# A macaron stack of four mixtures and attentions on one core: the first mixture's choices written in program order on every compute engine, and the bias table's row and pieces moved

## The chip, the cores and the metric

The kernel runs on one core of a Trainium2 chip. The metric is the device time of one execution in microseconds (us), the median of several runs; smaller is better. A core has five engines that run side by side and meet at semaphores: TensorE (PE in the profile; its weight loads are PEld), VectorE (DVE), ScalarE (ACT), GpSimd (POOL) and SyncE (SP), which issues most transfers. ScalarE and GpSimd can issue transfers too; all transfers are carried by the same 16 DMA engines.

## What is computed

The reference is a stack of four layers, each with a half-weighted feed-forward part, an attention part and a second half-weighted feed-forward part, on x of shape 4 x 512 x 128. The change touches the first feed-forward part and the preparation of the attention that follows it. Cut to these:

```python
def _L0_ffn_ref(inputs, gate_w, w1, b1, w2, b2):
    tokens = inputs.reshape(-1, d_model)
    capacity = int(np.ceil(CAP_FACTOR * T / num_experts))
    logits = jnp.einsum('td,ed->te', tokens, gate_w)
    probs = jax.nn.softmax(logits, axis=-1)
    expert_idx = jnp.argmax(probs, axis=-1)
    mask = jax.nn.one_hot(expert_idx, num_experts)
    ranks = jnp.cumsum(mask, axis=0) - 1.0
    keep = (ranks < capacity) * mask
    sec_mask = jax.nn.one_hot(ranks.astype(int), capacity) * keep[:, :, None]
    combine_weights = probs[:, :, None] * sec_mask
    dispatch = jnp.einsum('tec,td->ecd', sec_mask, tokens)
    h = jax.nn.relu(jnp.einsum('ecd,edh->ech', dispatch, w1) + b1[:, None, :])
    expert_out = jnp.einsum('ech,ehd->ecd', h, w2) + b2[:, None, :]
    return jnp.einsum('tec,ecd->td', combine_weights, expert_out)

# attention of layer 0: a bias table by distance, 16 heads
table = rel_pos_emb.reshape(2 * MAX_LEN - 1, H, D).sum(axis=-1)
bias = transpose(table[rel_idx]); att = q k / sqrt(D) + bias; causal softmax; att v

x = x + 0.5 * _L0_ffn_ref(_layernorm(x), ...)
x = x + _L0_attn_ref(_layernorm(x), ...)
x = x + 0.5 * _L0_ffn_ref(_layernorm(x), ...)
# layers 1 to 3 follow
```

So each token is normalised, chooses one of 8 experts, and gets the next free row of that expert, up to a capacity of 320.

## The kernel before

The kernel is written in a tile language: the author writes instructions on engines, and a scheduler puts the instructions of each engine into one fixed order and adds the waits. Within a `manual_schedule` block the engines named there keep the order of the program text. After the build each engine works through its own list in order, so an instruction that waits holds everything behind it on that engine. Transfers that SP issues go into one queue, and likewise those of ScalarE.

Four batches of 512 tokens (`NB`, `S`) lie in fast memory as four tiles of 128 tokens each (`NT`). The first mixture, `f00`, is an object of class `Mixture`:

- `empty` (L288) fills the rows of the dispatch buffer `disp_f` in device memory with zeros, `clear` (L293) the result rows `res_f`; both are transfers of SP (`spread_zeros`, L284).
- `tokens` (from L296) is a generator for one batch: statistics on VectorE (`norms`, L168 and L169), reciprocal root on GpSimd (L172, L173, and L176, L177 for the offset when ScalarE or GpSimd scales), the scaled rows (L182 on ScalarE, L186 on VectorE), a turn on TensorE (L195) with its copy (L321 or L134), the logits (L330), then the choice: maximum (L344), exponentials (L348), mask (L228 to L234), running count (L362), ranks on TensorE (L373, L375, L379), gate factor (L385 to L389), and the row number `to` (L400 to L409). Last, GpSimd copies the factor into the row (L413) and scatters the rows of four tiles to `disp_f`, one indirect transfer for each tile (L416). L307 writes the tokens' own numbers into a column of each row. It is used by every mixture of the kernel, in later stages too.
- `experts` (from L426) fetches an expert's rows (`fetch`, L447), turns them (L466) with a copy on ScalarE (L468), makes the list of places to send results to (L472, L475 on VectorE), multiplies by `w1` (L490), adds the bias and clips on ScalarE (L494) and VectorE (L495), multiplies by `w2` (L526), adds `b2` (L506), weights the rows (L511) and scatters them (L512). Expert e + 2 is fetched and e + 1 prepared while e is computed; an optional `beside` is called once for each expert.

`prep_table` (from L1012) makes the bias table of attention 0, again as a generator with three stops: it loads `rel` (L1016); sums it, turns it on TensorE (L1024), writes a row `tab_row` and stores it in device memory as `tab_rows` (L1032); then, for eight pairs of heads, loads a shifted piece `rev` (L1038, buffers shared under the name "raw", five of them), turns it with TensorE (L1043) and copies it into `table`. `copy` (L131) alternates between VectorE (L134) and ScalarE (L136). The left part of `table` is filled with zeros (L1020). `prep_l0_attn` loads and turns the attention's weights (L144 to L147, L976 to L988), and `padded_values` fills two value buffers `vpad` on GpSimd (L585, L586). `first_weights` loads the experts' weights in eight transfers (L563, L564) and turns the bias `b1` (L570, copied at L571 into `b1T`).

At the top of the program these are called in this order: the table's first stop, the fill of `disp_f`, four steps of batch 0's choice, the table's second stop, all weights, the fill of `res_f`, the rest of the choices with a lag of two steps between batches, the table's pieces, the attention weights, the value buffers, the experts. Batches 0 and 2 are scaled by ScalarE, 1 and 3 by VectorE. No block gives an order there; the scheduler does. Attention 0 (`l0_attn`) follows the experts and has its order written out.

Of the kernel before, what the change touches and what calls it, by code (L numbers as in the profile page):

```python
# [17 lines left out]
P = 128  # L18
D = 128
NB, S = 4, 512  # L20
# [3 lines left out]
E = 8  # L24
# [17 lines left out]
def kernel(ctx: ExitStack, tc: tile.TileContext, a: dict, out: bass.AP):  # L42
    nc = tc.nc
# [9 lines left out]
    def const(shape, name, dtype=FP):  # L53
        return cpool.tile(shape, dtype, name=name, tag=name)

    def bank(name):
        return psum.tile([P, 512], FP, name=name, tag="bank", bufs=8)
# [7 lines left out]
    xs = [const([P, NT, D], f"x{b}") for b in range(NB)]  # L65
# [58 lines left out]
    def load_row(ap, name, tag=None):  # L124
        t = pools["w"].tile([P, D], FP, name=name, tag=tag or name)
        nc.sync.dma_start(t, ap.partition_broadcast(P))
        return t
# [3 lines left out]
    def copy(dst, src):  # L131
        n_copies[0] += 1
        if n_copies[0] % 2:
            nc.vector.tensor_copy(dst, src)  # L134
        else:
            nc.scalar.copy(dst, src)  # L136
# [23 lines left out]
    def norms(srcs, dsts, tag, on="vector", fine=False):  # L160

        g = len(srcs) * NT
        st = small.tile([P, g, 6], FP, name=f"st_{tag}", tag=f"bn_st{g}")
        mv = small.tile([P, g, 2], FP, name=f"mv_{tag}", tag=f"bn_mv{g}")
        rs = small.tile([P, g], FP, name=f"rs_{tag}", tag=f"bn_rs{g}")
        rstd = small.tile([P, g], FP, name=f"rstd_{tag}", tag=f"bn_rstd{g}")
        for t in range(g):
            nc.vector.bn_stats(st[:, t, :], srcs[t // NT][:, t % NT, :])  # L168
            nc.vector.bn_aggr(mv[:, t, :], st[:, t, :])  # L169
            if fine and t % 2 and t < g - 1:  # L170
                yield
        nc.gpsimd.tensor_scalar(rs, mv[:, :, 1], EPS, None, ALU.add)  # L172
        nc.gpsimd.tensor_tensor(rstd, rs, mhalf[:, :g], ALU.pow)  # L173
        if on != "vector":
            off = small.tile([P, g], FP, name=f"off_{tag}", tag=f"bn_off{g}")
            nc.gpsimd.tensor_scalar(off, mv[:, :, 0], -1.0, None, ALU.mult)  # L176
            nc.gpsimd.tensor_tensor(off, off, rstd, ALU.mult)  # L177
        yield
        for t in range(g):
            src, dst = srcs[t // NT][:, t % NT, :], dsts[t // NT][:, t % NT, :]  # L180
            if on == "scalar" or (on == "both" and t % 2):
                nc.scalar.activation(dst, src, AF.Identity, bias=off[:, t : t + 1], scale=rstd[:, t : t + 1])  # L182
            elif on == "gpsimd":
                nc.gpsimd.tensor_scalar(dst, src, rstd[:, t : t + 1], off[:, t : t + 1], ALU.mult, ALU.add)
            else:
                nc.vector.tensor_scalar(dst, src, mv[:, t, 0:1], rstd[:, t : t + 1], ALU.subtract, ALU.mult)  # L186
            if fine and t % 2 and t < g - 1:
                yield
        yield
# [55 lines left out]
    class Mixture:  # L245
# [50 lines left out]
        def tokens(self, bs, wT, on="vector", pool=None, fine=False, apart=False):  # L296

            pool = pool or routing
            k, G = self.k, len(bs) * NT
            i0 = bs[0] * NT  # L300
            tag = f"{self.tag}_{bs[0]}"

            ns = [work.tile([P, NT, W + 2], FP, name=f"n_{self.tag}_{b}", tag="nm", bufs=4) for b in bs]
            rows = [n[:, :, 2 : 2 + D] for n in ns]
            for n, b in zip(ns, bs):
                for c in range(k):
                    nc.gpsimd.tensor_scalar(  # L307
                        n[:, :, 0 if c else D + 2],
                        tok_id[:, c * TILES + b * NT : c * TILES + (b + 1) * NT],
                        1.0,  # L310
                        None,
                        ALU.add,
                    )
            yield from norms([xs[b] for b in bs], rows, tag, on, fine)
            if fine:
                yield
            nTs = []
# [37 lines left out]
            if k == 2:  # L355
                rest = without(pool, pr, by_tile[0], G, -4.0, f"r{G}")
                _, second = route(pool, rest, G, f"r1{G}", by_tile[1])
# [14 lines left out]
            ps = bank(f"rank_{tag}")[:, : k * E * G]  # L372
# [7 lines left out]
            ps = ps.rearrange("p (k e g) -> p k e g", k=k, e=E)  # L380
# [202 lines left out]
    def padded(pool, i):  # L583
        v = pool.tile([P, NT, NH, SLOT], FP, name=f"vpad{i}", tag=f"vpad{i}", bufs=1)
        nc.gpsimd.memset(v, 0.0)  # L585
        nc.gpsimd.memset(v[:, :, :, HD : HD + 1].rearrange("p t h o -> p (t h o)"), 1.0)  # L586
        return v

    def padded_values(pool):
        vpads[:] = [padded(pool, i) for i in range(2)]  # L590
# [419 lines left out]
    l0 = {}  # L1010

    def prep_table(pool):  # L1012


        rel = stage.tile([P, D], FP, name="rel", tag="rel", bufs=1)
        nc.sync.dma_start(rel, a["L0_attn_rel_pos_emb"][P - 1 : 2 * P - 1, :])  # L1016
        yield

        table = pool.tile([P, NH, S], FP, name="table", tag="table", bufs=1)
        nc.vector.memset(table[:, :, : S - 2 * P], 0.0)  # L1020
        tab = stage.tile([P, NH], FP, name="tab", tag="tab", bufs=1)
        nc.vector.tensor_reduce(tab, rel.rearrange("p (h d) -> p h d", d=HD), AX.X, ALU.add)
        ps = bank("tabT")
        nc.tensor.matmul(ps[:NH, :P], tab, flip, start=True, stop=True)  # L1024
        last = stage.tile([NH, 1], FP, name="tab_last", tag="tab_last", bufs=1)
        nc.vector.tensor_copy(last, ps[:NH, 0:1])
        row = stage.tile([NH, 3 * P], FP, name="tab_row", tag="tab_row", bufs=1)
        nc.vector.memset(row[:, :P], 0.0)
        nc.vector.tensor_scalar(row[:, P : 2 * P], ps[:NH, :P], last, None, ALU.subtract)
        nc.vector.memset(row[:, 2 * P :], NEG)  # L1030
        rows = dram.tile([NH, 3 * P], FP, name="tab_rows", tag="tab_rows")
        nc.sync.dma_start(rows, row)  # L1032
        yield

        for h in range(0, NH, 2):

            rev = stage.tile([P, 2, 2 * P], FP, name=f"rev{h}", tag="raw")
            nc.sync.dma_start(  # L1038
                rev,
                bass.AP(tensor=rows.tensor, offset=rows.offset + h * 3 * P, ap=[[1, P], [3 * P, 2], [1, 2 * P]]),  # L1040
            )
            ps = bank(f"turned{h}")
            nc.tensor.matmul(ps, flip, rev.rearrange("p h s -> p (h s)"), start=True, stop=True)  # L1043
            copy(table[:, h : h + 2, S - 2 * P :], ps.rearrange("p (h s) -> p h s", h=2))
        l0["table"] = table
        yield

    def prep_l0_attn():
        qkv = head_weights(a["L0_attn_qkv_w"], a["L0_attn_qkv_b"], "l0")
        owT = load_T(a["L0_attn_proj_w"], D, D, "ow0T", "owT")  # L1050
        ob = load_row(a["L0_attn_proj_b"], "ob0", "ob")
        l0["attn"] = qkv, owT, ob
# [533 lines left out]
    def whole(parts):  # L1586
        for _ in parts:
            pass

    def skewed(gens, lag):  # L1590

        live = {i: g for i, g in enumerate(gens)}
        r = 0
        while live:
            for i in list(live):
                if r >= i * lag and next(live[i], "end") == "end":
                    del live[i]
            r += 1
            yield
# [16 lines left out]
    def first_weights():  # L1616
        l0["w"] = yield from moe_weights("L0_ffn", "l0")

    pairs = [[b, b + 1] for b in range(0, NB, 2)]
    gate0T = wpool.tile([D, E], FP, name="gate0T", tag="gate0T")  # L1620
    ps = bank("gate0T")
    nc.tensor.transpose(ps[:, :E], gate0, ident[:E, :E])
    nc.vector.tensor_copy(gate0T, ps[:, :E])
    with tc.tile_pool(name="tables", bufs=1) as tables:
        f00 = Mixture("f00", CAP0, 1)
        f00.zeroed(stage, "raw", 5)
        made = prep_table(tables)
        next(made)
        whole(f00.empty())
        with tc.tile_pool(name="routing00", bufs=2) as pool:  # L1630
            choices = [f00.tokens([b], gate0T, "vector" if b % 2 else "scalar", pool) for b in range(NB)]
            for part in choices[:1] * 4:
                next(part)
            next(made)
            whole(first_weights())
            f00.clear()
            whole(skewed(choices, 2))
        whole(made)
        prep_l0_attn()
        padded_values(tables)  # L1640
        f00.experts(l0["w"])
        f01 = Mixture("f01", CAP0, 1)

        f30 = Mixture("f30", CAP3, 2)
        l0_attn(f00.combine, emptied(f01, f30), lambda b: f01.tokens([b], gate0T, fine=True))
    with tc.tile_pool(name="weights12", bufs=1) as mid:
        pools["w"] = mid
        prep_l1()
        with tc.tile_pool(name="raw2", bufs=1) as pool:
            made = prep_l2(pool)  # L1650
# [119 lines left out]
```

## Time and profile before

| What | us |
|---|---|
| Median of 3 runs (1506.3 to 1509.8) | 1507.57 |
| The profiled execution | 1509.34 |
| Its span in the profile | 1507.4 |
| TensorE busy in the span | 1284.4 (85%) |
| VectorE busy | 873.8 (58%) |
| ScalarE busy | 686.4 (46%) |
| GpSimd busy | 691.8 (46%) |
| Mean granted TensorE clock, of 1 | 0.911 |

The first stretches of the span, in busy microseconds of each engine:

| Stretch, us | TensorE | VectorE | ScalarE | GpSimd | granted clock | DMA, GB/s |
|---|---|---|---|---|---|---|
| 0 to 20 | 1.87 | 14.03 | 4.20 | 12.63 | 1.00 | 242 |
| 20 to 40 | 15.14 | 8.69 | 2.84 | 8.25 | 1.00 | 268 |
| 40 to 60 | 11.06 | 4.23 | 1.76 | 8.09 | 0.78 | 125 |
| 60 to 80 | 19.36 | 6.78 | 7.73 | 6.19 | 0.96 | 70 |
| 80 to 100 | 20.00 | 7.01 | 9.26 | 10.21 | 1.00 | 60 |
| 100 to 120 | 8.68 | 5.98 | 3.87 | 7.96 | 0.82 | 48 |

The choices of the first mixture lie in 4 to 51 us, its experts in 62 to 112, and attention 0 begins behind them. A group of the page is named by line, engine, operation and tile; a line of the chain gives start, length and the piece of work; a line of the timeline gives start, length, engine, line, operation, tiles, and in brackets the idle time of the engine just before it and what ended that. Busy time is an average over stages: which engine sets the pace is read from the waits of a stage, not from these columns.

### The profile page before, as it was taken

The numbers are of one execution on the slowest core, as the hardware profiler recorded it, in microseconds if no ns is written. First come the engines' busy times: TensorE is split into PE (matmuls) and PEld (weight loads), VectorE is DVE, ScalarE is ACT, GpSimd is POOL, SyncE is SP. The second block draws the span as 40 slices with busy tenths as digits, with TensorE's granted clock in tenths as the row PEclk, the third lists the DMA queues.
The fourth block names the chain that finished last, engine by engine and source line by source line (L and its number), as shares of the span: only waits on it lengthen the run. The fifth ranks groups of instructions, "written<-read, shape, count | busy, mean of one in ns | idle before, by whom it ended". The sixth has DMA issues, their size and how long they took to land.

```text
span 1507.4 us, 28892 instructions
## 1 busy us (share of the span) xinstructions
PE 1284.4 (85%) x10677; PEld 828.3 (55%) x10677; DVE 873.8 (58%) x2934; ACT 686.4 (46%) x1439; POOL 691.8 (46%) x808
## 2 busy tenths in 40 slices
PE   4787999995979989998999878749599999998394
PEld 3464666674766666676656656627343434333273
DVE  5336777663345657777566655434287787772243
ACT  1235877871433367776622222104245555553041
POOL 5355767871433577876442112555502323202243
PEclk9898999996979999999999877859799999997597
DMA  8410240002412884241130000032105000000223
GB/s 259 106 53 22 80 170 13 9 5 75 146 42 58 231 257 137 93 141 31 38 76 1 1 0 3 29 91 85 49 8 184 8 12 4 16 1 15 78 82 108
DMA packets 100660, 106.21 MB, mean 70 GB/s; under 512 B 9084, under 2 KB 73832, under 8 KB 100520
## 3 DMA queue, kind: packets, MB, share of 16 engines
q1 hardware_dynamic: 91752, 90.11, 20.7%
q0 software_dynamic: 6656, 13.22, 2.5%
q8 instruction: 84, 1.38, 0.4%
q10 hardware_dynamic: 2112, 1.05, 0.3%
q14 instruction: 56, 0.46, 0.1%
HBM read 62.49 MB, written 41.85 MB: 69 GB/s over the span
## 4 chain that ended last, share of the span: by engine, by line
PE 67%; DVE 10%; POOL 7%; issue 6%; DMA 6%; ACT 2%; SPq 1%; POOLq 0%; DVEq 0%; ACTq 0%
PE s_a L621 13%; PE t_a L666 9%; PE h_f L490 5%; PE acc_a L688 5%; PE o_f L526 5%; PE acc_a L826 5%; PE y_f L1451 4%; PE t_a L621 3%; PE ot_a L845 2%; POOL res_f L512 2%; PE gate_f L1468 2%; DMA cb_f<-rows_f 2%; POOL disp_f L416 1%; PE lg_f L330 1%; PE T_f L195 1%
## 5 line engine op out<-in xcount | busy, mean ns | idle before, releaser
L653 POOL TENSOR_SCALAR sc_a<-sc_a,top_a 128x128 f32<-128x128 f32 (+3 forms) x256 | 275.9, 1093 | 87.1 <-DVE top_a L638 60.2
L621 PE MATMUL s_a<-k_a,q_a 32*128 32x512 f32 (+3 forms) x1536 | 264.1, 537 | 5.3 <-DVE top_a L642 4.5
L710 DVE TENSOR_REDUCE low<-s_a 128x1 f32<-128x512 f32 x256 | 163.0, 683 | 42.7 <-PE t_a L621 30.4
L730 ACT ACTIVATE w_a<-t_a 128x512 f32<-128x512 f32 x240 | 131.8, 596 | 108.1 <-PE t_a L621 68.7
L666 PE MATMUL t_a<-ident,sc_a 128*128 128x128 f32 x1280 | 171.3, 279 | 4.9 <-DVE top_a L642 4.1
L512 POOL DMA_INDIRECT res_f<-y_f,back_f x112 | 106.9, 954 | 129.1 <-ACT y_f L511 94.2
L666 PEld LDWEIGHTS t_a<-ident,sc_a 128*128 128x128 f32 x1280 | 142.4, 142 | 39.9 <-issue 16.6
L621 PE MATMUL t_a<-ql_a,k_a 32*128 32x512 f32 x480 | 158.8, 644 | 0.4 <-DVE low L710 0.3
L655 ACT ACTIVATE sc_a<-sc_a,top_a 128x128 f32<-128x128 f32 (+3 forms) x256 | 134.8, 576 | 15.3 <-DVE top_a L642 14.8
L621 PEld LDWEIGHTS s_a<-k_a,q_a 32*128 32x128 f32 x1536 | 93.8, 185 | 73.3 <-issue 38.4
L675 ACT ACTIVATE w_a<-t_a 128x256 f32<-128x256 f32 (+2 forms) x192 | 94.2, 526 | 68.9 <-PE t_a L666 68.5
L416 POOL DMA_INDIRECT disp_f<-n_f,to_f x96 | 94.8, 987 | 52.8 <-issue 36.9
L526 PE MATMUL o_f<-w_l,h_f 128*128 128x128 f32 (+1 forms) x896 | 110.4, 278 | 1.4 <-ACT h_f L494 1.0
L526 PEld LDWEIGHTS o_f<-w_l,h_f 128*128 128x128 f32 (+1 forms) x896 | 102.2, 184 | 10.4 <-DVE back_f L475 4.4
L490 PE MATMUL h_f<-dT_f,w_l 128*128 128x320 f32 (+1 forms) x256 | 105.1, 549 | 2.8 <-ACT dT_f L468 2.8
L172 POOL TENSOR_SCALAR rs_f<-mv_f 128x4 f32<-128x4 f32 (+1 forms) x23 | 5.3, 230 | 205.5 <-DVE mv_f L169 202.0
L688 PE MATMUL acc_a<-w_a,vpad 128*32 128x128 f32 x2560 | 97.4, 277 | 0.6 <-ACT w_a L675 0.6
L677 ACT COPY w_a<-t_a 128x256 f32<-128x256 f32 (+2 forms) x192 | 93.5, 527 | 4.4 <-PE t_a L666 4.4
L642 DVE CUSTOM_DVE_ANT_0 sc_a<-s_a,future 128x128 f32<-128x128 f32 (+3 forms) x128 | 62.3, 487 | 46.7 <-PE s_a L621 38.2
L642 DVE CUSTOM_DVE_ANT_0 sc_a<-s_a,table 128x128 f32<-128x128 f32 (+3 forms) x128 | 62.3, 486 | 43.7 <-PE s_a L621 33.3
L511 ACT ACTIVATE y_f<-o_f,d_f 128x128 f32<-128x128 f32 (+1 forms) x112 | 39.0, 394 | 103.4 <-DVE o_f L506 94.2
L826 PE MATMUL acc_a<-w_a,vpad 128*32 128x256 f32 x1024 | 83.6, 397 | 2.7 <-ACT w_a L730 2.4
(347 smaller groups left out, 2258.4 us busy)
## 6 DMA issues: line engine op xcount, KB each, us to landing
fac_a<-fac_a_sb SPq DMA_DIRECT2D x36, 256.0 KB
disp_f<-zeros_f SPq DMA_DIRECT2D x4, 2080.0 KB
d_f<-disp_f SPq DMA_DIRECT2D x32, 260.0 KB
w_l<-in_L_ffn_w_dram SPq DMA_DIRECT2D x16, 512.0 KB
cb_f<-rows_f SPq DMA_DIRECT2D x16, 512.0 KB
q_a<-fac_a SPq DMA_DIRECT2D x32, 256.0 KB
k_a<-fac_a SPq DMA_DIRECT2D x32, 256.0 KB
r_f<-res_f SPq DMA_DIRECT2D x16, 256.0 KB
```

Source lines behind the costliest of these rows:

```text
L490: nc.tensor.matmul(ps[u][:, :cap], w1[:, e, (c + u) * P : (c + u + 1) * P], dT, start=True, stop=True)
L512: nc.gpsimd.indirect_dma_start(out=self.back[e * per + s][:, :], out_offset=bass.IndirectOffsetOnAxis(ap=back[:m, s : s + 1], axis=0), in_ ...
L526: nc.tensor.matmul(po[:m, s, :], h[:, c, s * P : s * P + m], w2[:, e, c, :], start=(c == 0), stop=(c == NC - 1),)
L621: nc.tensor.matmul(ps[:, n0:n1], q[r : r + SLOT, i * P : (i + 1) * P], k[r : r + SLOT, n0:n1], start=True, stop=True)
L642: nc.vector.tensor_tensor_reduce(sc, banks[r][:, :n], more, -1.0, HUGE, ALU.add, ALU.min, top)
L653: nc.gpsimd.tensor_scalar(sc, sc, top, None, ALU.subtract)
L655: nc.scalar.activation(sc, sc, AF.Exp, bias=top, scale=-1.0)
L666: nc.tensor.transpose(ps[:, x * n + j * P : x * n + (j + 1) * P], st["sc", u, i, r0 + x][:, j * P : (j + 1) * P], ident,)
L688: nc.tensor.matmul(st["acc", u][r * SLOT : (r + 1) * SLOT, i * P : (i + 1) * P], vpads[b % 2][:, j, g * 4 + r, :], st["w", u, i, r][:, j * ...
L710: nc.vector.tensor_reduce(st["low", u][:, i, c : c + 1], ps, AX.X, ALU.max, negate=True)
L730: nc.scalar.activation(w, ps, AF.Exp)
L826: nc.tensor.matmul(acc[r * SLOT : (r + 1) * SLOT, n0:n1], vpads[b % 2][:, j, g * 4 + r, :], st["w", u, j, r, half] if ("w", u, j, r, half) ...
```

## The change

In the text of the first mixture: `tokens` writes the number column after `norms` instead of before it. The choices, the table, the bias `b1` and the value buffers stand in a block in which TensorE, VectorE, ScalarE and GpSimd keep the program's order. All weight loads and the fill of `res_f` are issued first; all four batches are scaled by ScalarE; the choices run with a lag of two steps, and after eight steps of that the table's row is made, then the rest of the choices, then the pieces, then `b1`, then the value buffers. The eight pieces are loaded through ScalarE's queue, all copied by VectorE, and the table's zero part is filled after them. The attention weights are prepared from within `experts`, at the second expert's `beside`.

```diff
@@ -302,6 +302,7 @@
             ns = [work.tile([P, NT, W + 2], FP, name=f"n_{self.tag}_{b}", tag="nm", bufs=4) for b in bs]
             rows = [n[:, :, 2 : 2 + D] for n in ns]
+            yield from norms([xs[b] for b in bs], rows, tag, on, fine)
             for n, b in zip(ns, bs):
                 for c in range(k):
                     nc.gpsimd.tensor_scalar(
...
-            yield from norms([xs[b] for b in bs], rows, tag, on, fine)
@@ -1017,7 +1017,6 @@
         table = pool.tile([P, NH, S], FP, name="table", tag="table", bufs=1)
-        nc.vector.memset(table[:, :, : S - 2 * P], 0.0)
         tab = stage.tile([P, NH], FP, name="tab", tag="tab", bufs=1)
@@ -1035,13 +1034,14 @@
             rev = stage.tile([P, 2, 2 * P], FP, name=f"rev{h}", tag="raw")
-            nc.sync.dma_start(
+            nc.scalar.dma_start(
                 rev,
...
             nc.tensor.matmul(ps, flip, rev.rearrange("p h s -> p (h s)"), start=True, stop=True)
-            copy(table[:, h : h + 2, S - 2 * P :], ps.rearrange("p (h s) -> p h s", h=2))
+            nc.vector.tensor_copy(table[:, h : h + 2, S - 2 * P :], ps.rearrange("p (h s) -> p h s", h=2))
+        nc.vector.memset(table[:, :, : S - 2 * P], 0.0)
         l0["table"] = table
@@ -1627,18 +1627,33 @@
         whole(f00.empty())
-        with tc.tile_pool(name="routing00", bufs=2) as pool:
-            choices = [f00.tokens([b], gate0T, "vector" if b % 2 else "scalar", pool) for b in range(NB)]
-            for part in choices[:1] * 4:
-                next(part)
+        E_ = mybir.EngineType
+        with (
+            tc.tile_pool(name="routing00", bufs=2) as pool,
+            tc.manual_schedule(engines={E_.PE, E_.DVE, E_.Activation, E_.Pool}),
+        ):
+            weights = first_weights()
+            for _ in range(E // 2):
+                next(weights)
+            f00.clear()
+            choices = skewed([f00.tokens([b], gate0T, "scalar", pool) for b in range(NB)], 2)
+
+            for _ in range(2 * NB):
+                next(choices)
             next(made)
-            whole(first_weights())
-            f00.clear()
-            whole(skewed(choices, 2))
-        whole(made)
-        prep_l0_attn()
-        padded_values(tables)
-        f00.experts(l0["w"])
+            whole(choices)
+            whole(made)
+            whole(weights)
+            padded_values(tables)
+
+        def behind_expert():
+
+            yield
+            prep_l0_attn()
+            yield
+
+        beside = behind_expert()
+        f00.experts(l0["w"], lambda _: next(beside, None))
```

`skewed` steps the generators in turn, each starting `lag` rounds after the one before it; it is as it was:

```python
def skewed(gens, lag):
    live = {i: g for i, g in enumerate(gens)}
    r = 0
    while live:
        for i in list(live):
            if r >= i * lag and next(live[i], "end") == "end":
                del live[i]
        r += 1
        yield
```

## The prediction

> **What bounds it now.** I read the chain of waits in order of time first, since it says which stretch sets the end. The diff touches the first 66 us; the chain runs through them engine by engine and only afterwards through TensorE without a gap.
>
> ```profile
> 26.52 1.88 PE lg_f L330 x8
> 43.04 0.96 POOL disp_f L416
> 51.98 0.45 SPq L447
> 52.45 4.53 DMA rev<-tab_rows
> 57.11 3.75 PE turned L1043 x4
> 60.87 0.65 PE ps_wqkvT_l L147 x3
> 63.00 2.42 PE h_f L490 x8
> 65.84 1.98 PE o_f L526 x16
> 71.62 1.98 PE o_f L526 x16
> ```
>
> Columns: start, length, piece. From 65.84 on an expert takes 5.78 us (65.84 to 71.62) and TensorE sets it. Before that, three things follow each other: 16 scatters on GpSimd, then the fetch of rows (SPq L447), then the last two pieces of the table and the attention weights (52.45 to 61.8). The timeline of GpSimd shows why the scatters are late:
>
> ```profile
> 7.20 1.80 POOL L585 MEMSET vpad<- 128x2048 f32 x1
> 10.29 1.05 POOL L173 TENSOR_TENSOR rstd_f<-rs_f,mhalf 128x4 f32<-128x4 f32 x1
> 12.29 1.80 POOL L585 MEMSET vpad<- 128x2048 f32 x1
> 14.06 0.20 POOL L177 TENSOR_TENSOR off_f<-off_f,rstd_f 128x4 f32<-128x4 f32 x1
> 29.68 1.24 POOL L416 DMA_INDIRECT disp_f<-n_f,to_f  x1 [5.54 <-DVE masks_f L234]
> 49.55 0.96 POOL L416 DMA_INDIRECT disp_f<-n_f,to_f  x1 [0.30 <-issue]
> ```
>
> Two unrelated fills stand between the statistics of batch 0 (6.6) and its scale (14.26). From 29.68 to 50.51 GpSimd is full: 16 scatters, 1.26 apart, 20.8 us. So the first scatter sets the last one. VectorE's timeline has the rows that I price with:
>
> ```profile
> 1.96 3.47 DVE L1020 MEMSET table<- 128x4096 f32 x1 [0.79 <-issue]
> 42.96 0.68 DVE L134 COPY table<-turned 128x512 f32<-128x512 f32 x1
> 54.66 0.16 DVE L472 SCALAR_TENSOR_TENSOR lost_f<-d_f,astray 128x3 f32<-128x3 f32 x1 [8.57 <-DMA d_f<-disp_f]
> 64.38 0.55 DVE L495 TENSOR_SCALAR h_f<-h_f,b1T_l 128x320 f32<-128x320 f32 x1 [1.66 <-PE h_f L490]
> ```
>
> And the stretches, whose PEclk column is the granted TensorE clock:
>
> ```profile
> 52.00:54.00 2.00, 0.00 (x0) 0.00 (x0) 0.00 (x0) 0.00 (x0) 0.00 (x0) 0.50 0.42 111
> 60.00:61.00 1.00, 1.00 (x4) 0.38 (x3) 0.00 (x0) 0.10 (x1) 0.00 (x0) 0.50 0.53 141
> 61.00:62.00 1.00, 1.00 (x7) 0.57 (x5) 0.45 (x1) 0.51 (x2) 0.00 (x0) 0.74 0.44 129
> 62.00:63.00 1.00, 0.36 (x3) 0.14 (x2) 0.72 (x7) 0.67 (x2) 0.54 (x2) 1.00 0.83 244
> ```
>
> TensorE idles from 48.9, falls to half clock, is busy again at 57.11 and gets the full clock near 61.5: 4.4 us at half. Today this falls on table work, and the experts start warm.
>
> **The change, part by part.** The order in which the built program's instructions stand on each engine is known, so I walk it with the rows' durations.
>
> *Choices in program order.* Without the table fill VectorE starts on x0 when it lands (4.4 instead of 5.37). Strict statistics cost 0.40 a tile (116.31 to 117.82 in attention): batch 0 ends at 6.1, batch 1 at 7.7. GpSimd: sum 0.23, power 1.05, offset two of 0.2, with waits 2.0: scale ready at 8.1, not 14.26. From there the chain costs what it does now: 14.30 to 22.04 held a queueing gap, so by pieces: scale and transposes 2.2, copy 0.6, logits 1.9, hence VectorE's first maximum at 12.9. Batches 1 and 3 are scaled on ScalarE instead of VectorE: eight operations of 0.41, 3.3 us, in time that ScalarE spends waiting, and two more offsets on GpSimd (0.9 us, counted in the 2.0 of each batch). Batches 2 and 3 have their statistics behind the masks of 0 and 1: masks 0 end 14.1, statistics of 2 15.7; logits of 1 at 16.5, masks 1 end 17.7, statistics of 3 19.3. GpSimd's scale of batch 3 (2.0) stands ahead of the first scatter: 19.3 + 2.0 + 0.45 for the counts' copy and its wait = 21.75. The slots are ready at 20.1, and the fill of the rows (issued at 5.48) has 4.3 MB up to its end; at the 280 GB/s of this stretch it is through near 18.5. So the first scatter is at 21.75 instead of 29.68. Slots of 1, 2 and 3 come at about 26.2, 30.0 and 33.5, and GpSimd wants them at 27.4, 32.7 and 38.0; no gap. Four groups of 5.05 and three borders of 0.3 to 0.7 put the last scatter at 41.85 instead of 49.55: 7.7 earlier. An error of 1 us either way is what I give this walk.
>
> *Fetch and VectorE's queue.* The fetch goes out 2.43 after the last scatter (49.55 to 51.98): 44.28. Rows land 2.68 after issue now; three fetches of 195 KB in a row, 0.48 apart, end near 48.1. Here the change adds a wait: on VectorE the three L472 stand ahead of seven of the eight table copies, the 3.47 fill and the copy of b1T (L571), and the first h_f needs b1T. Seven copies at 0.61 (starts of equal 128x512 operations in attention) are 4.3; start 48.5, copies to 52.85, fill to 56.25, b1T to 56.5. TensorE meanwhile waits for banks that these copies free, and has transposed the rows and made h of expert 0 by 53.5. First o_f at 57.1, against 65.84: 8.7 earlier. The fill cost nothing at the front in the end (scale was late anyway) and 3.4 here.
>
> *Attention weights* move behind expert 1's rows, into a stretch TensorE fills: 60.66 to 61.78 was 1.1 at mixed clock; about 0.9 inside the experts. Before it also lay on the path, so I counted it out in the 8.7 and back here.
>
> *Clock.* TensorE has a gap from 53.5 to 57.1 after sparse work, so o_f starts at half clock. By the rows above 4.4 us pass at half: 2.2 lost. Bounds: 0 if it is warm, 2.8 by the 5.5 us of half clock after 1424.76 (6.42 for eight h_f against 3.44 later).
>
> [...]
>
> *Table.* The row is written behind eight weight loads and the second fill: 3.15 MB more, which took 24.7 to 34.2 before; started at once from 21.8 they end near 31.5, the row near 33. Eight pieces on ScalarE's queue: issue 0.53 each (four in 2.12 at 1492.76). The built waits make the fourth wait for the first and the eighth for the fourth, so three landings of 2.6 (fetch at 70.70 to 73.34) to 4.9 (piece at 42.74 to 47.7) follow each other: last piece turned at 42.5 to 49. It is due on VectorE at 52.2 and ahead of expert 0's transposes at 49.2, which have 3 us of slack. Cost 0; beyond that each microsecond costs one. ScalarE stands in this queue, but its next work is the dT copy at 50.
>
> *Hidden moves.* Two vpad fills (4.2 on GpSimd) now follow the scatters; GpSimd has nothing until the first y_f near 60; uncovered they cost 4.2. Small loads (4.9 us of SP issue: biases, gate, gamma, beta) stand ahead of the fetch but are through by 35. The column of counts (L307, 0.23 each, 20 behind this mixture) changes place on GpSimd, where attention and chain are led by TensorE: 0, bounds 0.5 either way. Everything else behind the first mixture stands in the same order on all engines, so the shift reaches the end.
>
> **Sum.** −8.7 + 0.9 + 2.2 = −5.6 on the profiled execution: span 1507.4, with 1.9 around it 1509.34. That one is 1.8 above the median of 1507.57; the shift is taken over to the median: 1502.0. Between the bounds (walk 1, landing 0.7, clock 0 to 2.8): 1499.3 to 1504.
>
> **Rivals.** *Warm clock*: the paced h and dT work of 49.2 to 53.5 keeps the full clock through the gap. For: 4 us of nearly busy time. Against: the clock fell 2.4 us after the last work at 48.9 (mean 0.82 in 50 to 52, 0.50 after it). Time 1499.8.
>
> *Late table*: row at 38 instead of 33 and slow landings, so the eighth piece holds TensorE until 54 and o_f until 60. For: it waits behind every load in one queue. Against: scatters move only 53 KB/us then. Time about 1505.
>
> *Fill shares the queue* (the slower side): with all weight loads issued at once, the fill of the rows, on which the first scatter waits, lands with the last of 8.4 MB, 30.8 at 280 to 290 GB/s; first scatter at 31.2, 9.4 later than I say: −5.6 + 9.4 = +3.8, 1511.4. It decides from a first scatter at 27.4. For: those loads used to stand behind a wait until 23.66. Against: rel, issued behind x at 3.38, had landed at 7.95, when about 1.4 MB had moved and over 4 MB were issued: in order.
>
> *It does not do what it says*: the build puts seven copies behind the fetch, so the table is not put in place while rows are scattered; this is in my sum. Were they through earlier, 4.3 more would be gained: 1497.7.
>
> **Numbers.** Forecast 0.60, warm clock 0.17, late table 0.12, shared queue 0.08, copies early 0.03. A measurement of this kernel tells 0.2% (3.0 us) from no change: faster is below 1504.55. Faster: 0.57 + 0.17 + 0.03 + 0.03 of the late table = 0.80; same 0.12; slower 0.08. Range 1498.0 to 1505.5 leaves out the shared queue and the ends.
>
> **What would show it.** First L416 at 21.75 and last at 41.85; SPq L447 at 44.3; VectorE: L472, seven copies, a 3.47 fill, L571, then L495 at 56.5; first o_f near 57 at clock 0.50 and 1.00 from 61.5; experts 5.78 apart. I am wrong if the first scatter waits for a DMA, if TensorE stands at a table piece after 49, or if the shift at expert 1 is not found at the end.

## The result, and the profile after

| | Before | After |
|---|---|---|
| Median of 12 runs, us | 1507.96 (1502.58 to 1510.31) | 1506.69 (1501.18 to 1509.77) |
| Ratio | 1 | 0.9987, 95% interval 0.9975 to 0.9999 |
| Profiled execution, us (its span) | 1509.34 (1507.4) | 1503.93 (1502.2) |
| Last scatter starts, us of the span | 49.55 | 43.26 |
| First fetch issued | 51.98 | 47.91 |
| First product with `w2` (o_f) | 65.84 | 61.83 |
| The same of the last but one expert | 100.49 | 98.86 |
| Results fetched (L541) | 112.87 | 111.25 |

1507.96 times 0.0013 is 2.0 us less (0.2 to 3.8); the medians differ by 1.3. That is about a third of the forecast 5.6 and within the 0.2% set as no change. The two profiled spans differ by 5.2, but runs of one kernel spread over 8 us. The steadier measure is where the same work stands in the trace: at the last two lines of the table it is 1.6 us earlier, for the reasons below. Behind the first mixture the lead of the trace wanders (1.2 us at 346, 4.5 at 450, 5.2 at the end of the span); no run explains that part.

First the chain of waits of the changed kernel (start, length, piece), the answer to the first fence of the prediction:

```profile
21.98 1.24 POOL disp_f L416
...
31.64 4.13 DMA disp_f<-n_f,to_f
...
43.26 0.96 POOL disp_f L416
44.23 1.83 POOL vpad L585
46.31 1.71 POOL vpad L585
48.35 0.48 SPq L447
48.87 3.45 DMA d_f<-disp_f
52.71 4.19 DVE table L1043 x7
56.90 0.80 issue
57.70 3.47 DVE table L1044
61.25 0.54 ACT h_f L494
61.83 3.66 PE o_f L526 x16
...
70.19 1.79 PE o_f L526 x16
```

The first scatter is where it was expected. Then a landing of scattered rows is on the chain (31.64), two fills seem to stand between the last scatter and the fetch, and behind the landing VectorE works for 8.5 us before the first h_f. The first 16 o_f take 3.66, 1.98 before. The timeline has the moments that the prediction named:

```profile
12.92 0.19 DVE L344 TENSOR_REDUCE mx_f<-lg_f 128x4 f32<-128x32 f32 x1 [3.22 <-PE lg_f L330]
...
33.18 0.17 DVE L409 TENSOR_TENSOR to_f<-slot_f,spare_f 128x4 int32<-128x4 f32 x1 [2.01 <-DMA disp_f<-n_f,to_f]
...
47.91 1.45 SPq L447 DMA_DIRECT2D d_f<-disp_f  x3
...
50.47 0.16 DVE L472 SCALAR_TENSOR_TENSOR lost_f<-d_f,astray 128x3 f32<-128x3 f32 x1 [9.51 <-DMA d_f<-disp_f]
...
52.35 0.16 DVE L472 SCALAR_TENSOR_TENSOR lost_f<-d_f,astray 128x3 f32<-128x3 f32 x1 [0.84 <-DMA d_f<-disp_f]
```

12.92 was forecast as 12.9. The slots of batch 2 wait 2.01 for the landing of batch 0's rows, which use the same buffer. The fetch goes out 4.65 after the last scatter's start (47.91 − 43.26), where 2.43 was taken over from before. The windows show the clock of TensorE (the column of 1.00 or 0.50):

```profile
60.00:61.00 1.00, 0.00 (x0) 0.00 (x0) 1.00 (x1) 0.12 (x1) 0.00 (x0) 1.00 0.00 0
61.00:62.00 1.00, 0.17 (x1) 0.17 (x2) 0.89 (x4) 0.75 (x2) 0.00 (x0) 1.00 0.00 0
62.00:63.00 1.00, 1.00 (x6) 1.00 (x7) 0.33 (x1) 0.20 (x1) 0.00 (x0) 0.50 0.03 8
...
64.00:65.00 1.00, 1.00 (x6) 1.00 (x6) 0.00 (x0) 0.00 (x0) 0.00 (x0) 0.50 0.00 0
65.00:66.00 1.00, 1.00 (x6) 0.84 (x5) 0.42 (x1) 0.01 (x1) 0.00 (x0) 0.80 0.00 0
```

TensorE waits from 59.66 to 61.83 for VectorE; the clock halves at 62.0, as the experts begin, and is back at 65.4.

### The profile page after: what moved, and what is told of

It reads as the page before. It is cut to its first block, busy times and chain, and to the rows that moved or that the text cites. A ratio compares the mean times of both kernels' runs of the same rounds, so it can differ in the third digit from the quotient of the medians.

```text
span 1502.2 us, 28899 instructions
## 1 busy us (share of the span) xinstructions
PE 1282.0 (85%) x10677; PEld 827.0 (55%) x10677; DVE 875.5 (58%) x2929; ACT 688.7 (46%) x1444; POOL 694.4 (46%) x812
## 4 chain that ended last, share of the span: by engine, by line
PE 70%; DVE 10%; POOL 7%; DMA 5%; issue 5%; ACT 3%; SPq 0%; POOLq 0%; another core or an unknown queue 0%; ACTq 0%; DVEq 0%
PE s_a L621 13%; PE t_a L666 9%; PE o_f L526 6%; PE h_f L490 6%; PE acc_a L688 5%; PE acc_a L826 5%; PE y_f L1451 4%; PE t_a L621 3%; POOL disp_f L416 2%; PE ot_a L845 2%; PE gate_f L1468 2%; PE o_f L1253 1%; PE T_f L195 1%; PE gu_f L1218 1%; PE qk_a L996 1%
## 5 line engine op out<-in xcount | busy, mean ns | idle before, releaser
L526 PEld LDWEIGHTS o_f<-w_l,h_f 128*128 128x128 f32 (+1 forms) x896 | 103.8, 186 | 12.9 <-ACT h_f L494 5.4
```

Of the source, the lines that this page charges most:

```text
L526: nc.tensor.matmul(po[:m, s, :], h[:, c, s * P : s * P + m], w2[:, e, c, :], start=(c == 0), stop=(c == NC - 1),)
```

## The experiments

All were derived from the changed kernel and compared with the kernel before on the chip that ran them. The chips differ (median before: 1486.6 beside e1 to e4, 1488.7 beside e16, 1509.2 to 1509.7 beside the others), so ratios count, and the places of events in one trace of each. "Distance" is from the last scatter's start to the fetch's issue; o_f 7 is the first o_f of the last but one expert, by the timeline.

| Kernel | First scatter | Last scatter | Fetch (distance) | First o_f (its 16) | o_f 7 | Ratio to before (95%) |
|---|---|---|---|---|---|---|
| before | 29.68 | 49.55 | 51.98 (2.43) | 65.77 (2.05) | 100.42 | 1 |
| changed | 21.98 | 43.26 | 47.91 (4.65) | 61.83 (3.66) | 98.79 | 0.9987 (0.9975 to 0.9999) |
| e1 fills moved | 25.16 | 45.88 | 50.54 (4.66) | 61.24 (3.65) | 98.18 | 0.9982 (0.9966 to 0.9999) |
| e2 four pieces | 23.66 | 45.03 | 47.48 (2.45) | 61.64 (2.05) | 96.97 | 0.9986 (0.9972 to 1.0) |
| e3 zeros moved | 25.27 | 46.66 | 51.36 (4.70) | 59.91 (2.05) | 95.24 | 0.9955 (0.994 to 0.9969) |
| e4 four slots | 21.99 | 42.10 | 47.05 (4.95) | 62.02 (3.53) | 98.98 | 0.9995 (0.9979 to 1.0011) |
| e5 zeros behind | 23.48 | 45.10 | 49.90 (4.80) | 62.06 (2.05) | 97.39 | 0.9987 (0.997 to 1.0005) |
| e7 half weights | 21.99 | 43.06 | 47.24 (4.18) | 57.60 (2.2) | 92.93 | 0.9961 (0.9943 to 0.9979) |
| e8 e5 and e7 | 22.10 | 43.17 | 47.20 (4.03) | 55.60 (2.05) | 90.93 | 0.9931 (0.991 to 0.9951) |
| e9 e8, four slots | 22.46 | 42.62 | 47.40 (4.78) | 56.82 (2.05) | 92.15 | 0.9947 (0.9927 to 0.9966) |
| e10 e8, row by ScalarE | 21.93 | 42.84 | 46.85 (4.01) | 55.26 (2.05) | 90.59 | 0.9962 (0.9945 to 0.998) |
| e13 table as before | 22.22 | 43.77 | 48.59 (4.82) | 55.41 (2.05) | 90.75 | 0.9949 (0.9932 to 0.9966) |
| e15 e8, kept busy | 22.31 | 43.04 | 46.44 (3.40) | 53.29 (2.05) | 88.62 | 0.9952 (0.9932 to 0.9971) |
| e16 all together | 21.87 | 42.76 | 46.30 (3.54) | 54.76 (2.05) | 90.08 | 0.9922 (0.99 to 0.9943) |

(e7's 16 products stand in two parts, 0.94 and 1.28.)

**What makes the fetch late: e1 and e2.** e1 moves the fills, e2 leaves out half the pieces (its table holds the fourth piece again in their place):

```diff
             whole(weights)
-            padded_values(tables)
...
             prep_l0_attn()
             yield
+            padded_values(tables)
+            yield
```

> The two fills of padded values (4.1 us on GpSimd) go from behind the last scatter to the third expert. The changed kernel issues its fetch 4.65 us after the start of its last scatter (43.26 to 47.91), the kernel before 2.43. Theory 'fills': GpSimd's fills hold up the last scatters' end, so the distance falls to 2.4 and the fetch is issued near 45.7. Theory 'pieces': the last scatters' rows share the DMA engines with the second four pieces of the table (1 MB, 45.0 to 49.1), so the distance stays 4.6 +- 0.4. Either way the build of this kernel puts six of the table's eight copies on VectorE ahead of the first L472, one behind it, and the last, the fill of zeros and the copy of b1T behind the third L472. So behind the third landing VectorE has 0.6 + 3.5 + 0.1 instead of 4.3 + 0.8 + 3.5 + 0.1: by 'pieces' third landing 52.4, first o_f near 57.2 (61.83 now), the later experts 4 to 5 us earlier; by 'fills' near 55.2, 6 to 7 us earlier. Rival: TensorE's own work ahead of the first o_f (two turns of rows and eight products at half clock, 5.7 us from the first turn, 53.52 now) sets it: then not before 56.

```diff
-            rev = stage.tile([P, 2, 2 * P], FP, name=f"rev{h}", tag="raw")
-            nc.scalar.dma_start(rev, ...)
+            if h < NH // 2:
+                rev = stage.tile([P, 2, 2 * P], FP, name=f"rev{h}", tag="raw")
+                nc.scalar.dma_start(rev, ...)
```

> Only the first four pieces of the table are fetched (1 MB instead of 2); the last four products take the fourth piece's rows again, so the bias of heads 8 to 15 is another's. Order on all engines unchanged but for the four DMA issues on ScalarE's queue. 'Pieces': DMA engines are free when the last scatters' rows go out, the fetch is issued 2.4 after the last scatter's start, near 45.7, and the third landing comes with it, so first o_f and the later experts are 2.2 to 3 us earlier. 'Fills': distance stays 4.65, nothing changes beyond 0.3 us at the experts.

The timelines of GpSimd and SP, e1 first:

```profile
6.28 1.79 POOL L585 MEMSET vpad<- 128x2048 f32 x1
8.06 1.05 POOL L173 TENSOR_TENSOR rstd_f<-rs_f,mhalf 128x4 f32<-128x4 f32 x1
...
45.88 0.96 POOL L416 DMA_INDIRECT disp_f<-n_f,to_f  x1 [0.30 <-issue]
...
50.54 1.46 SPq L447 DMA_DIRECT2D d_f<-disp_f  x3
```

```profile
45.03 0.96 POOL L416 DMA_INDIRECT disp_f<-n_f,to_f  x1 [0.30 <-issue]
...
47.48 1.45 SPq L447 DMA_DIRECT2D d_f<-disp_f  x3
```

With no fill behind the scatters (e1) the distance is 4.66; with the fills there and half the pieces gone (e2) it is 2.45. So "fills" falls, although the chain of waits had drawn them between scatter and fetch: that chain goes by what ended last in time, not by what was waited for. The transfers of the stretch behind the last scatter (44 to 48 of the changed kernel, then 45 to 48 of e2) show what shares the engines:

```profile
q10 hardware_dynamic: 772, 0.73, 63.7%
q0 software_dynamic: 78, 0.16, 10.4%
```

```profile
q0 software_dynamic: 64, 0.13, 13.2%
```

q0 carries the scattered rows, q10 ScalarE's pieces: packets, MB, share of 16 engines. Both queues moved in the one stretch of the changed kernel, and only the rows' in that of e2; the price of the pieces here is 2.2 us (4.66 in e1, with 59.8% of the engines on q10 from 46 to 51, against 2.45).

e1 also did something that I hadn't expected: outside the ordered block the scheduler put the fills back between the statistics and the scale of batch 0 (6.28), where the kernel before had them. The first scatter is 3.2 later for it. That is what the new place of the fills is worth, and it is free behind the scatters. The forecast for e1's later experts, 4 to 5 us earlier, missed (0.6): the last scatter is 2.6 later, so the third landing came at 55.55 instead of 52.4, and the fill and b1T stand behind it.

e2 gave 1.8 us at the seventh expert (2.2 to 3 forecast) with a first scatter 1.7 later: its GpSimd waited 2.29 there though ScalarE, which the trace names, had finished batch 0 at 9.8. What remained to wait for, by elimination, was the fill of the rows by zeros. So the rival "shared queue" holds in part: the fill lands close to the moment when it is wanted, sometimes behind it (e2, e5).

**The slots' wait: e4.**

```diff
-            tc.tile_pool(name="routing00", bufs=2) as pool,
+            tc.tile_pool(name="routing00", bufs=4) as pool,
```

> The slots' tile gets four buffers instead of two, so slots of batch 2 and 3 no longer wait for the landing of batch 0's and 1's scatters (2.01 and 0.93 us on VectorE); order on all engines unchanged. Theory: third group of scatters starts at 32.8 instead of 34.19, last scatter 41.9 instead of 43.26, fetch 1.4 earlier, all later work 1.4 earlier. Rival 'pieces' sharpened: the fetch waits for the DMA engines, which the pieces (45.0 to 49.1) hold whenever the scatters are issued; then last scatter is 1.4 earlier but the fetch only 0 to 0.5, and the time is the same.

```profile
47.05 0.92 SPq L447 DMA_DIRECT2D d_f<-disp_f  x2
...
51.39 0.16 DVE L472 SCALAR_TENSOR_TENSOR lost_f<-d_f,astray 128x3 f32<-128x3 f32 x1 [8.90 <-DMA d_f<-disp_f]
```

The last scatter is 1.16 earlier, the fetch 0.86, but the rows land 0.92 later than in the changed kernel, because the pieces are still coming, and the experts gain nothing. The wait that stood on the chain at 31.64 was worth 0: the pieces bind behind it.

**The work behind the landing on VectorE: e3, e5, e13.** e3 and e5 move the table's fill to GpSimd, at the third expert or in order behind the padded values:

```diff
-        nc.vector.memset(table[:, :, : S - 2 * P], 0.0)
         l0["table"] = table
...
             padded_values(tables)
+            nc.gpsimd.memset(l0["table"][:, :, : S - 2 * P], 0.0)
```

> The table's fill of zeros (3.47 us, VectorE, 57.70 to 61.17) goes to GpSimd at the third expert. The build now also puts six copies ahead of the first L472, one behind the first, one and b1T's copy behind the second. Theory 'VectorE's queue sets the start of the experts': h_f gets b1T near 51.5, and first o_f is set by TensorE: turn of rows near 50.7, eight products at half clock 4.1, second turn 0.6: first o_f near 56.5 instead of 61.83, and because TensorE has no gap ahead of it, its 16 matmuls take 2.0 and not 3.66: later experts 5.3 to 7 us earlier. Rival 'fetch bound': the landing is later with nothing else to wait for it and only 3.5 + 0.8 are won.

> Only the table's fill of zeros moves, from VectorE to GpSimd, in program order behind the two fills of padded values; everything else stands as in the changed kernel. The earlier try (zeros at the third expert) was built with the fill at the front, between batch 0's statistics and scale, and its first scatter was 3.3 us late; here it can't be. Theory 'the fill and 0.8 before it are the whole': 4.3 us of VectorE's queue go, b1T near 56.9, first o_f near 57.6 (61.83). Rival 'TensorE is next': two turns of rows and eight products at half clock end at 59.7, so first o_f is at 59.8, 2.0 earlier, and as TensorE then has no gap its 16 matmuls take 2.0 instead of 3.66: later experts 3.7 earlier. Fetch 4.6 after the last scatter's start in both.

e3 was built with the fill at 6.26, in front, and its first scatter is 3.3 late; its later experts are 3.6 earlier, not 5.3 to 7. Counted from the fetch, e5's first o_f comes after 12.16 us (62.06 − 49.90), the changed kernel's after 13.92: 1.8 less, not 4.3, since TensorE is next (its products end at 61.7). And its 16 products take 2.05, as there is no gap: 3.4 in all from the fetch, forecast 3.7 for the rival. At the seventh expert only 1.4 of it is left, because e5's first scatter came 1.5 late, by elimination for the zeros of the rows again:

```profile
POOL disp_f L416 <- ACT n_f L182: 2.2, 1, 2.2
```

(the waits: who, for what, us, times, longest.) e13 writes the table's making as it was and keeps the rest of the change:

```diff
+        nc.vector.memset(table[:, :, : S - 2 * P], 0.0)
         tab = stage.tile([P, NH], FP, name="tab", tag="tab", bufs=1)
...
-            nc.scalar.dma_start(
+            nc.sync.dma_start(
...
-            nc.vector.tensor_copy(table[:, h : h + 2, S - 2 * P :], ...)
-        nc.vector.memset(table[:, :, : S - 2 * P], 0.0)
+            copy(table[:, h : h + 2, S - 2 * P :], ...)
```

> The changed kernel with the table's making put back as it was: zeros filled by VectorE at the front, pieces by SP's queue, copies in turn by VectorE and ScalarE. Choices in program order, attention weights behind expert 0 and padded fills behind the scatters stay. The build puts four copies on VectorE ahead of the first L472, four on ScalarE, and b1T behind the first L472; nothing of 8 us stands behind the fetch any more. Theory 'VectorE's queue took the gain back': the fill costs the choices at most 1 us (their first scatter waits for zeros of rows near 22 anyway), pieces still hold the DMA engines, fetch 4.6 after the last scatter near 48 to 49, first o_f by turn, copy, eight products and turn 5.7 behind the first landing, 56 to 57.5, 2.0 for 16 matmuls: later experts 6 to 7 us ahead of the changed kernel's. Rival 'ScalarE's queue is what brings the pieces early': SP issues them behind small loads and ahead of the fetch, so the fetch is late by pieces still waiting, 52 or more, and the experts are not earlier.

```profile
51.38 0.16 DVE L472 SCALAR_TENSOR_TENSOR lost_f<-d_f,astray 128x3 f32<-128x3 f32 x1 [1.31 <-DMA d_f<-disp_f]
51.66 0.18 DVE L571 COPY b1T_l<-b_l 128x32 f32<-128x32 f32 x1
...
51.40 0.61 PE L466 MATMUL dT_f<-ident,d_f 128*128 128x128 f32 x3 [0.55 <-ACT table L136]
52.65 2.42 PE L490 MATMUL h_f<-dT_f,w_l 128*128 128x320 f32 x8 [0.64 <-ACT dT_f L468]
...
55.41 2.05 PE L526 MATMUL o_f<-w_l,h_f 128*128 128x128 f32 x16
```

The fill isn't at the front here: the program's order put it at 21.02, ahead of the row, where it holds batch 1's slots, and the second group of scatters waits 1.71. So the fetch is 0.7 later than in the changed kernel (48.59), the last piece is turned 1.6 later (at 50.7), and yet the first o_f is 6.4 earlier and the seventh expert 8.0: b1T is there 0.3 after the first landing, and behind TensorE's wait of 0.55 the eight products take 2.42, as they do at a clock of 1.00 in e15. So in the traces the part of the change that moved the table cost 8 us at the experts (by the ratios, 0.9987 and 0.9949, 5.7), and the rest of the change is the gain.

**Getting it back: e7 to e10.** e7 asks for the weights of experts 4 to 7 behind the choices (`range(E // 4)` for `range(E // 2)`); e8 adds e5's edit, e9 e4's to that, e10 instead the row by ScalarE's queue.

> Experts 4 to 7's weights (2.1 MB) are asked for behind the choices instead of ahead of the zeros of the results and the table's row. The build then puts all eight copies of the table, the fill and b1T ahead of the first L472 on VectorE. Theory 'order': copies, fill and b1T are done before the rows land, the table's pieces come some 4 us earlier, the fetch goes out 2.5 to 4.6 after the last scatter, and first o_f follows the first landing by turn 0.6, copy 0.6, eight products 4.1, turn 0.6: 54.5 to 56.5 instead of 61.83, with 2.0 instead of 3.66 for its 16 matmuls, so later experts 7 to 9 us earlier. Rival 'moved weights': the same bytes now share the DMA engines with pieces and last scatters, fetch no earlier than 47.9, fill still behind the eighth copy near 51, b1T near 55: first o_f 56.5, later experts 7 earlier at most, and less where the loads come ahead of the rows.

> Both: weights as in the run before, zeros of the table on GpSimd behind the padded values. If the fill is off the path there already ('order'), same experts within 0.5 us; if b1T is what the first h_f waits for there, up to 3.5 us earlier.

> The run before with four buffers for the slots. With all weights asked for at once this made the last scatter 1.2 us earlier and the fetch no earlier, because the pieces held the DMA engines. Theory: with the pieces ahead of the scatters' end it is worth what it takes from VectorE's wait, up to 1.4 us at the fetch and at the experts. Rival: landings are quick now and the wait is gone, or the DMA engines are still full: 0.

> Zeros of the table on GpSimd, half the weights behind the choices, and now the table's row also by ScalarE's queue, so that it isn't behind weights in SP's. If queues share the DMA engines evenly, the row lands before 30 instead of near 33, the last piece near 44 instead of 47, the fetch goes out 2.5 after the last scatter instead of 4.0, and first o_f is 1.5 earlier than 55.6. Rival: the row waits for the engines all the same (2 to 3 MB of weights are ahead of it on each), nothing changes; or pieces now hold up scatters 4 to 8, on which slots of batches 2 and 3 wait, and the last scatter is later by what the fetch gains.

In e7 all copies, the fill and b1T precede the landing's work as built, and the seventh expert is 5.9 earlier, below the theory's 7 to 9 and within the rival's 7 at most:

```profile
52.16 0.13 DVE L571 COPY b1T_l<-b_l 128x32 f32<-128x32 f32 x1
...
54.13 0.55 DVE L495 TENSOR_SCALAR h_f<-h_f,b1T_l 128x320 f32<-128x320 f32 x1 [1.71 <-PE h_f L490]
...
57.60 0.94 PE L526 MATMUL o_f<-w_l,h_f 128*128 128x128 f32 x6 [0.94 <-ACT h_f L494]
```

b1T is not what the first h_f waits for: VectorE's waits for TensorE's products (54.13), and ScalarE's, for which o_f waits, starts at 57.01, in the built order behind the second copy of rows (56.69). e8 takes the fill away as well: 7.9. Of the 2.0 between them 1.3 is in the first turn and products (0.95 and 4.63 against 0.61 and 3.72; 0.96 and 4.63 in e9 at a clock of 0.50); the rest goes with ScalarE's order, since in e8 its first h_f stands ahead of that copy (52.07, 55.71). So e8's gain is not by the wait for b1T that its expectation names.

Distances are 4.0 to 4.2 in e7, e8 and e10 and 4.78 in e9. From 44 to 47 the DMA engines' share was 0.99, 1.05 and 0.64 in e8 (0.45, 0.70 and 0.22 in e9), and the first attention weights, 192 KB, now go out ahead of the fetch (42.58 in e7, 44.02 in e8; 49.48 in the changed kernel). That transfers still hold the rows up, but no longer the pieces alone, is my estimate; no run takes them apart.

e9 shows again that the slots' wait is not on the path. It is 1.2 behind e8: its clock fell at 49.8, ahead of the first turn, and turn and products ran at half clock throughout (0.96 and 4.63); in e8 it fell at 52.2 (0.61 and 3.72). In e10 the first `turned` comes at 34.72 instead of 35.95, but the last ends at 47.6 instead of 48.0 and the distance is 4.01 as in e8: what the row gains from the other queue is nearly gone by the last piece. Its ratio is 0.003 above e8's though its trace is 0.3 us ahead; the intervals overlap, and differences among the last six rows of the table are not told by the timing, but for e10 and e16, whose intervals just miss each other.

**The clock: e15.**

```diff
             whole(weights)
+            warm = bank("warm")
+            for _ in range(2):
+                nc.tensor.matmul(warm, flip, l0["rev"].rearrange("p h s -> p (h s)"), start=True, stop=True)
```

> Zeros on GpSimd and half the weights behind the choices, and two more products of the table's last piece into a bank that nobody reads (2.2 us of TensorE, from about 48.0). Theory 'clock': in that kernel without them TensorE waited 1.83 us ahead of the first turn and its eight products took 3.72; kept busy to 50.2 it holds the full clock, products take 2.4 to 2.7 and first o_f is 1.0 to 1.3 earlier than 55.6, less up to 0.3 by which the products hold up the turn. Rival: the clock falls all the same in the 0.64 us of the copy or is not what makes the products slow: no gain, and 0.3 lost.

TensorE's timeline, e8 and then e15:

```profile
49.98 0.61 PE L466 MATMUL dT_f<-ident,d_f 128*128 128x128 f32 x3 [1.83 <-DMA d_f<-disp_f]
51.23 3.72 PE L490 MATMUL h_f<-dT_f,w_l 128*128 128x320 f32 x8 [0.64 <-ACT dT_f L468]
```

```profile
45.79 1.98 PE L1648 MATMUL warm<-rev,flip 128*128 128x512 f32 x4
49.28 0.61 PE L466 MATMUL dT_f<-ident,d_f 128*128 128x128 f32 x3 [1.51 <-DMA d_f<-disp_f]
50.52 2.42 PE L490 MATMUL h_f<-dT_f,w_l 128*128 128x320 f32 x8 [0.64 <-ACT dT_f L468]
```

The products take 2.42 instead of 3.72, as the theory said, and the first o_f is 2.3 earlier, 0.8 of it from an earlier fetch. But the pieces were through at 45.6 in this run, so the added work ended at 47.8 and TensorE still waited 1.51 and the clock stayed at 1.00 up to 60, while in e1 the wait before the same turn was 0.99 and the clock fell at 54.4. So the length of this wait alone does not decide. The added products are 1.98 of the 2.77 us that TensorE worked from 45 to 49. That they kept the clock up is my estimate; one run is no proof.

**All together: e16.** e8, with pieces by SP's queue and copies in turn as in e13.

> Choices in program order as in the changed kernel, with what the runs before found: pieces by SP's queue and copies by VectorE and ScalarE in turn as in the kernel before, zeros of the table on GpSimd behind the padded values, half the weights behind the choices. First scatter 22, last 43; pieces through near 46, fetch 2.5 to 4.0 after the last scatter's start, 45.5 to 47; nothing but b1T on VectorE behind the first landing; first o_f 5.7 behind a landing at 48.1 to 49.6 where TensorE comes in cold, 4.1 where it is warm: 52.2 to 55.3 (61.83 in the changed kernel, 65.84 before). Against the kernel before: 10.5 to 13.5 us less, ratio 0.991 to 0.993. Rival: SP holds the fetch behind pieces that wait for TensorE, fetch 48.5 as in the run with the table as before, and it is no better than that: 0.995.

Fetch at 46.30 (distance 3.54), first o_f at 54.76, ratio 0.9922: in the forecast ranges, though at the late end for the o_f (products 3.94, against 2.42 in e15). It has the lowest ratio of all, clearly below the changed kernel's; from e8 and e15 it is not told apart.

## Why the prediction was wrong, step by step

**Right:** the mechanism and most terms. First maximum 12.92 (12.9), first scatter 21.98 (21.75), copies 4.27 (4.3), fill 3.47 (3.4), attention weights 0.88 between 69.31 and 70.19 (0.9), experts 5.77 apart, shift kept to the end of the mixture (1.6 at L541 as at the experts). The built order that puts seven copies and the fill behind the fetch was in the sum. That the first scatter fits within 0.2 is in part luck: the fill of the rows, put at 18.5, seems to come when it is wanted or later (first scatter 21.9 to 22.5 in nine runs, 23.5 and 23.7 in e5 and e2).

**The step that failed** is "The fetch goes out 2.43 after the last scatter". It took a distance from a stretch where only two pieces were still to come and nothing but the rows moved (0.13 MB from 49.55 to 51.98), and the step on the table had costed the pieces at 0, since it looked for them on TensorE and VectorE only. They were as late as its upper bound (last one turned at 49.1) and paid on the DMA engines: 4.65 (e1, e2). "GpSimd wants them at 27.4, 32.7 and 38.0; no gap" failed as well, by 1.4 at the third group, as the slots of batch 2 wait for a landing that the walk left out, but that error cost nothing by itself (e4). Together 3.6 at the fetch. Behind it a third landing that took 0.5 more and 0.80 of idle time ahead of the fill, less 0.2 in the last steps: 1.1 more. 57.1 became 61.83: 4.7 of the 8.7 gone. None of the prediction's three signs of being wrong looks at the stretch between scatter and fetch.

The 0.80 could have been read beforehand: the prediction's own row of the fill carries "[0.79 <-issue]", and every run with that fill on VectorE has it.

**Sizes off:** the clock cost 3.66 − 1.98 = 1.7, not 2.2. −4.0 + 0.9 + 1.7 = −1.4, against −1.6 in the trace. The prediction's bounds of 1499.3 to 1504 do not add up from its terms either: taken all one way they give 1498.1 to 1504.3.

The 4.4 us behind the 2.2 were read rightly, but they did not carry over. In the kernel before the clock came back at 61.5, 4.4 behind the start of the work at 57.11; in e2 at 59.9, 5.0 behind 54.92; in the changed kernel it fell at 62.0, just as the experts began, and was back at 65.4, after 3.4, as in the windows above. Measured between 40 and 130 us, the clock changed at 51.8, 58.6, 62.0, 65.4, 109.8 and 123.4 in the changed kernel and at 51.3, 61.5, 112.7 and 126.4 in the kernel before. In the 3.41 us ahead of its fall at 62.0 TensorE had worked 1.24 (58.59 to 62.00), and 1.84 ahead of e1's at 54.4 (51 to 54.4).

**Hidden moves** were right: fills behind the scatters cost nothing (e1's distance is the same without them). **The rivals:** "late table" named the right late thing and the wrong victim: TensorE's turn of expert 0 did wait until 53.5, but (by the order of events; the trace names no copy) for banks that VectorE's copies freed, and it cost nothing: b1T came 1.4 after the second turn. "Warm clock" did not come. "Copies early" had put 4.3 on the table's place in VectorE's queue; e13 shows 8.0 for copies, fill and clock together.

**Open:** how e16's ratio splits between its parts, how much of the distance in e7 to e10 belongs to pieces and how much to attention weights, and what sets the moments at which a run's clock changes.

## What to carry to other kernels

When a transfer is moved into an emptier stretch, ask which other transfer is due there, not only which engine reads it: the gap between a scatter and a fetch was 4.66 or 2.45 us here, with and without the pieces on the DMA engines (e1, e2). When a producer gets earlier, look at what the build now queues behind its consumer's wait; here 8 us of table work, which attention reads from 126 us on, stood between the landing and the first bias. And a piece on the chain of waits is a candidate, not a cause: two of them, the padded fills and the slots' landing, were worth nothing when taken away.

## What the hardware showed beyond that

All of this is read from the clock and work columns of the windows of these traces. The clock of TensorE read 1.00 or 0.50, and in the kernel before its 35 changes, in the changed kernel its 43, lay whole multiples of 3.41 us apart within 0.05. Up to 130 us, the 3.41 us ahead of a fall held 0 to 1.24 us of TensorE's work (five falls; 1.84 in e1), those behind the first fall that kept full clock 2.75 and more. At half clock, the 3.41 us ahead of a return held 2.83 to 3.41 (five returns), and those with up to 2.11 left it there. Later these sums do not tell: the clock fell at 836.35 after 3.17 of 3.41 us of work and stayed at half at 440.40 after 3.41 (kernel before), and fell at 519.38 after 3.06 (changed kernel). So no amount of work that decides is shown, and none for a wait: one of 0.99 stood ahead of a fall, one of 1.51 did not (e1, e15). Ahead of a trace's first change the clock column is no guide: in the kernel before it reads 1.00 up to 51.29, while the weight loads of equal `turned` products start 0.85 apart up to 44.21 and 0.43 from 44.77 on.

A fill of 128x4096 on VectorE had 0.79 or 0.80 us of idle time ahead of it in every run that has it there (both kernels, e1, e2, e4, e7, e13), which its 3.47 does not include. And the first scatter, which by elimination waits for the zeros of the rows, stood at 21.99 in one run and at 23.66 in another (e4, e2) with the same instructions up to there.
